# Layer 1's u and v by two levels of block products between layer 2's products, with weight factors read from DRAM and x kept there

## The chip, the cores and the metric

One Trainium2 chip, one core. The time is device microseconds (us) of one execution of the whole program, the median of three runs. Everything that is computed in matrix products here is fp32, except layer 3's sign products.

## The reference, cut to what matters

x is 8 images of 512 channels by 1024 pixels (32 x 32), and four layers follow one another. The change touches layer 1 and the order of layers 1 and 2.

```python
# layer 1, per image; h = group_norm(x), N = 1024, C = 512
q = wq h + bq ; k = wk h + bk ; v = wv h + bv
attn = softmax(q^T k / sqrt(C))          # over the 1024 keys
x = x + wp (v attn^T) + bp
# layer 2, per image: three 128-row projections t, p, g of x, softmax attention of
# t and p, then z = Z_w att, folded batch norm, x = x + z
```

The kernel folds weights: `wu` = wk^T wq, so that the scores of layer 1 are h^T u with u = wu h + bias (512 x 1024), and `wo` = (wp wv)^T, so that v = h^T wo (1024 x 512) already carries the output projection. u and v are thus one product each with a 512 x 512 matrix, per image.

## The kernel before

Before the main part, a start of some 210 us loads x, makes layer 0's small products for all images, layer 0's spectral norms (`chain`, a row of small dependent products for each pair of images) and the folded weights (`product`, `sums_of`, in a generator `filler` that is drawn on between the steps of the first chain). All that lives in SBUF pools `a1` and `a2`, which are closed there; the main part's pools (`late`, `big`, `epool`, `small`) lie over the same addresses. `big` is opened with `reuse_waits="tile"`; the others wait for the closed pools as a whole.

Then the images go one after the other through `fast`, in the order 6, 7, 0, 1, ... 5. In `fast(n)`:

- `scores1`: layer 1's scores h^T u, four calls of `seven`, exponentials, their sums `esum`. Between its steps the second half of the last image's layer 3 (`rest3`), then the load of the next x and layer 0 of the next image (`enter`), and steps of the remaining chains are drawn.
- `make_v`: v, two calls of `seven` with products of 128x256. After its fourth step `inverse_sums` makes the reciprocals of `esum`.
- `values1`: v times the exponentials, 14 groups of four products; in its middle the next image is normalised (`normal`) and split (`split_h`).
- `project2`, `scores2`, `values2`, `close2`, `leave`: layers 2 and 3. Between their steps `fill()` draws steps of `make_u` for the next image. `scores1` of the next image needs all of u and its sums.

All of the large products but layer 2's later ones go through `seven`: one level of Strassen's scheme in Winograd's form. It makes seven products of quarter matrices where eight are needed plainly. `sums_of` makes the left factors S1 to S4 from the quarters of one matrix, `differences_of` the right factors T1 to T4 from those of the other; the seven results are combined in PSUM evictions (DVE, ACT, and one POOL add in each `seven`).

PSUM is one ring of eight banks in the main part (`bank()`). x is double buffered in SBUF (two tiles of 16 KB per partition). `uv` is one 16 KB tile that holds u, then v. `wu`, `wo` and their sums `su`, `so` stay in SBUF (28 KB per partition). The order of each engine's instructions is written out when the program is built, by the tile framework, from the order in the source and its own estimate of when each becomes ready; on the chip each engine works off its list in order. A result that is late on the chip stops what is behind it.

Of the kernel before, what the change touches and what calls it, by code (L numbers as in the profile page):

```python
# [16 lines left out]
P = 128  # L17
B = 8
# [63 lines left out]

@with_exitstack
def kernel(
# [23 lines left out]
    xpool = ctx.enter_context(tc.tile_pool(name="x", bufs=2))  # L108
# [9 lines left out]
    def quad():  # L118
        return psum["bank"].tile([P, 4, P], F32, tag="bank", name="quad")

    def bank():
        return psum["bank"].tile([P, HF], F32, tag="bank", name="bank")

    def psum_pools(stack, wides, banks):
        psum.clear()
        for name, n in (("wide", wides), ("bank", banks)):
            if n:
                psum[name] = stack.enter_context(
                    tc.tile_pool(name=f"{name}{n}", bufs=n, space=PSUM, reuse_waits="tile")
                )  # L130

    def load_x(b):
        t = xpool.tile([P, CC, N], F32, tag="x", name="xt")
        src = x[b].rearrange("(cc p) n -> p cc n", p=P)
        for cc in range(CC):
            nc.sync.dma_start(out=t[:, cc, :], in_=src[:, cc, :])
        return t
# [108 lines left out]
    wu = wpool.tile([P, CC, C], F32, tag="wu", name="wu")  # L246
    wo = wpool.tile([P, CC, C], F32, tag="wo", name="wo")
# [4 lines left out]
    su = wpool.tile([P, 3, 2, C // 2], F32, tag="su", name="su")  # L252
    so = wpool.tile([P, 3, 2, C // 2], F32, tag="so", name="so")
# [39 lines left out]
    def sums_of(a, more):  # L293

        a11, a12, a21, a22 = a
        s1, s2, s4 = more
        tt = nc.vector.tensor_tensor
        tt(s1, a21, a22, ALU.add)
        tt(s2, s1, a11, ALU.subtract)  # L299
        tt(a21, a11, a21, ALU.subtract)  # L300
        tt(s4, a12, s2, ALU.subtract)
        return {"A11": a11, "A12": a12, "A22": a22, "S1": s1, "S2": s2, "S3": a21, "S4": s4}

    def differences_of(b, more):

        b11, b12, b21, b22 = b
        t1, t2, t4, t3 = (list(more) + [b12])[:4]
        tt = nc.vector.tensor_tensor
        tt(t1, b12, b11, ALU.subtract)
        tt(t2, b22, t1, ALU.subtract)  # L310
        tt(t3, b22, b12, ALU.subtract)
        tt(t4, b21, t2, ALU.subtract)
        return {"B11": b11, "B21": b21, "B22": b22, "T1": t1, "T2": t2, "T3": t3, "T4": t4}
# [45 lines left out]
    def product_of(lt, rhs, view=None, parts=1):  # L359

        def term(ps, ka, kb, first, last):
            fresh = ps is None
            if fresh:
                ps = bank()
            w = HF // parts
            for q in range(parts):
                for k in range(2):
                    mm(  # L370
                        out=ps[:, q * w : (q + 1) * w],
                        lhsT=lt(ka, kb, q, k),
                        rhs=rhs(ka, kb, q, k),
                        start=first and q == 0 and k == 0,
                        stop=last and k == 1,
                        skip_group_check=True,
                    )
            return ps, ps if view is None else view(ps)

        return term  # L380
# [72 lines left out]
    def make_u(env, hb, got):  # L453

        ut = env["big"].tile([P, CC, N], F32, tag="uv", name="ut")
        wa = weights["u"]

        def done():
            us = env["big"].tile([P, 3, 2, HF], F32, tag="us", name="us")
            got.append(  # L460
                sums_of(quarters_of(ut, chunks, [half(0), half(1)]), [us[:, i] for i in range(3)])
            )

        for i in range(2):
            term = product_of(
                lambda a, b, q, k: wa[a][:, k, bass.ts(i, P)],
                lambda a, b, q, k: hb[b][:, k, :],
            )
            yield from seven(
                term,  # L470
                ut[:, i, half(0)],
                ut[:, i, half(1)],
                ut[:, 2 + i, half(0)],
                ut[:, 2 + i, half(1)],
                bu[:, i : i + 1],
                bu[:, 2 + i : 3 + i],
                then=done if i else None,
            )

    def make_v(hb, vt):  # L480

        wa = weights["o"]
        w = C // 2
        for i in range(0, NTH, 2):
            term = product_of(
                lambda a, b, q, k: hb[b][:, k, bass.ts(i + q, P)],
                lambda a, b, q, k: wa[a][:, k, :],
                lambda ps: ps.rearrange("p (q c) -> p q c", q=2),
                2,
            )  # L490
            lo, hi = slice(i, i + 2), slice(NTH + i, NTH + i + 2)
            yield from seven(
                term, vt[:, lo, 0:w], vt[:, hi, 0:w], vt[:, lo, w:], vt[:, hi, w:]
            )

    def scores1(env, hb, ua, es):
# [3 lines left out]
        for i in range(NTH):  # L500
            lo, hi = (env["e"].tile([P, N], F32, tag="e", name="e") for _ in range(2))
            es[i], es[NTH + i] = lo, hi
            term = product_of(
                lambda a, b, q, k: hb[b][:, k, bass.ts(i, P)],
                lambda a, b, q, k: ua[a][:, k, :],
# [14 lines left out]
    def values1(env, xt, vt, es, r, more):  # L520
# [4 lines left out]
        w = C // 2  # L525
        a11, a12, a21, a22 = quarters_of(
            vt, [slice(0, NTH), slice(NTH, NT)], [slice(0, w), slice(w, C)]
        )
        s2 = more[:, 0, :].rearrange("p (t c) -> p t c", c=w)
# [5 lines left out]
        def group(ps, a, e, r_, first, last):  # L535
            for t in range(NTH):
                mm(  # L537
                    out=ps,
                    lhsT=a[:, t, bass.ts(r_, P)],
# [6 lines left out]
        def scaled(dst, oc, h):  # L546

            nc.vector.tensor_tensor(dst, dst, r[:, h, :], ALU.mult)
            xs = xt[:, oc, half(h)]
            nc.gpsimd.tensor_tensor(xs, xs, dst, ALU.add)  # L550
# [10 lines left out]
        pa = [bank(), bank()]  # L561
# [9 lines left out]
        for i in range(2):  # L571
            group(pa[i], a12, e21, i, False, True)
            d = temp(1)
            tt(d, pa[i], r[:, 0, :], ALU.mult)
# [7 lines left out]
        for i in range(2):  # L582
            pb = bank()
# [3 lines left out]
        pc = [bank(), bank()]  # L587
# [11 lines left out]
        pd = [bank(), bank()]  # L599
# [12 lines left out]
    def project2(env, xt, made):  # L612
# [11 lines left out]
        term = product_of(lambda a, b, q, k: wa[a][:, k, :], lambda a, b, q, k: xb[b][:, k, :])  # L624
# [194 lines left out]

    def fast(env, n, hb, ua):  # L820
# [3 lines left out]
        xt = resident.pop(b)  # L824
        more = n + 1 < B
        ahead = iter(())
# [8 lines left out]
        for k, _ in enumerate(scores1(env, hb, ua, es)):  # L835
            if rest3 and k % 2:
                if next(rest3[0], "end") == "end":
                    rest3.pop()
                    if more and order[n + 1] not in resident:
                        resident[order[n + 1]] = load_x(order[n + 1])  # L840
# [8 lines left out]
        vt = env["big"].tile([P, NT, C], F32, tag="uv", name="vt")  # L849
        for k, _ in enumerate(make_v(hb, vt)):  # L850
            if k == 3:
                r = inverse_sums(env, esum, n)
            chore(2)
        scratch = env["big"].tile([P, 3, N], F32, tag="us", name="scratch")
        got = []
        steps = iter(())
        for k, _ in enumerate(values1(env, xt, vt, es, r, scratch)):
            chore(2)
            if k == 5 and more:
                nxt = resident[order[n + 1]]  # L860
                hb = split_h(env, normal(env, nxt))
        signs = None
        if more:
            steps = make_u(env, hb, got)
# [8 lines left out]
        for k, _ in enumerate(project2(env, xt, made)):  # L873
            fill(k > 5)
        tt, pt, gt = made
        es, esum = scores2(env, pt, tt, lambda t: fill(t % 2))
        banks, r = [None, None], None

        def values2(h, ts):
            if banks[h] is None:  # L880
                banks[h] = bank()
# [16 lines left out]
        fill()  # L898
# [4 lines left out]
        values2(1, range(0, NTH))  # L903
        close2(xt, att, 0)
        att = values2(1, range(NTH, NT))
        count = iter(()) if more else count_bad(env)
        next(count, None)
        fill()
        for _ in leave(env, xt, dst, [0], signs):
            fill()  # L910
        close2(xt, att, 1)
        fill(2)
# [7 lines left out]
        return hb, got[0] if more else None  # L920
# [387 lines left out]

    def filler():
# [5 lines left out]
        cols2 = [slice(0, C // 2), slice(C // 2, C)]  # L1315
        weights["u"] = sums_of(quarters_of(wu, chunks, cols2), [su[:, i] for i in range(3)])
        scale_z()
        yield
        yield from biases()
        for j in rest:  # L1320
            yield from grams(j)
        yield from product(nat["v"], sbw["p"], wo)
        weights["o"] = sums_of(quarters_of(wo, chunks, cols2), [so[:, i] for i in range(3)])
# [33 lines left out]
    with ExitStack() as main:  # L1357
        psum_pools(main, 0, 8)
# [3 lines left out]
        env.update({"big": big, "e": epool, "small": small})  # L1362
        got = []
        hb = split_h(env, normal(env, resident[order[0]], True))
        for _ in make_u(env, hb, got):
            pass
        ua = got[0]
# [36 lines left out]
    def general(env, xt, b, dst):  # L1404
        for _ in enter(xt, load_f(b), weights0(b)):
            pass
        ht = normal(env, xt)
        ut = env["big"].tile([P, CC, N], F32, tag="u", name="u")
        vt = env["big"].tile([P, NT, C], F32, tag="v", name="v")
        for oc in range(CC):  # L1410
            for h in range(NH):
                ps = bank()
                for cc in range(CC):
                    mm(
                        out=ps,
                        lhsT=wu[:, cc, bass.ts(oc, P)],
# [5 lines left out]
        for t in range(NT):  # L1422
            ps = bank()
            for cc in range(CC):
# [3 lines left out]
                    rhs=wo[:, cc, :],  # L1428
# [58 lines left out]
    with tc.If(verdict[0] > 0):  # L1487
        with (
# [7 lines left out]

            for a in (weights["u"], weights["o"]):
                nc.vector.tensor_tensor(a["S3"], a["A11"], a["S3"], ALU.subtract)
# [45 lines left out]
```

## Time and profile before

| | |
|---|---|
| median of 3 runs | 1959.05 us (1958.59 to 1959.05) |
| the profiled execution: its time, its span | 1959.65 us, 1957.9 us |
| PE, weight loads, DVE, ACT, POOL busy | 1913.9, 989.2, 1151.2, 512.8, 223.9 us |
| one image in the middle (from one `values1` to the next, 784 to 997 us) | 212.4 us |
| DMA | 67.0 MB in all |

Line numbers such as L370 are those of the kernel before. L370 is the product inside `product_of`, so the products of u, v, layer 1's scores and layer 2's projections all carry it, and are told apart by the tiles they read. An fp32 product shows as two PE records. [...]the pace is read from a long row of them in the chain of waits, where a row of 112 records in 48.07 us is 0.429 us for each record.

### The profile page before, as it was taken

Reading aid. Unit: us, or ns where it says so; the run is one execution under the profiler, and the core shown is the slowest. Engines: PE = TensorE matmul, PEld = TensorE weight load, DVE = VectorE, ACT = ScalarE, POOL = GpSimd, SP = SyncE. Lnnn points to the kernel's source line nnn. Section 1 sums busy time; section 2 is a strip of 40 time slices with the busy share of each in tenths; the row PEclk is TensorE's granted clock in tenths of the full one; section 3 lists DMA queues with packets and bytes.
Section 4 is the critical chain, followed back from the end, with each engine's and each line's share of the span. In section 5 each row is a group of like instructions: output and inputs, shape, how many; then the busy total and the mean of one; then the engine's idle time right before and its main releaser. Section 6 shows DMA issues by size and latency. Waiting matters only on the chain.

```text
span 1957.9 us, 16696 instructions
## 1 busy us (share of the span) xinstructions
PE 1913.9 (98%) x6230; PEld 989.2 (51%) x6230; DVE 1151.2 (59%) x1859; ACT 512.8 (26%) x811; POOL 223.9 (11%) x176
## 2 busy tenths in 40 slices
PE   8999899999999999999999999999999999999997
PEld 2377347454565446454455446444645445544653
DVE  3245667537774487637754577447663775466546
ACT  2132122125220342024211332025202421134114
POOL 1000001300021001210112001200120011201110
PEclk9989899999999999999999999999999999999999
DMA  9320000002000020001100120002000110010001
GB/s 337 130 76 1 6 6 12 1 11 86 6 12 1 11 86 17 1 1 46 56 11 0 33 70 12 1 11 86 11 0 1 51 46 11 0 33 22 11 1 56
DMA packets 26712, 66.99 MB, mean 34 GB/s; under 512 B 3760, under 2 KB 4016, under 8 KB 25984
## 3 DMA queue, kind: packets, MB, share of 16 engines
q1 hardware_dynamic: 25968, 65.09, 9.8%
q8 instruction: 51, 0.84, 0.2%
q0 software_dynamic: 224, 0.33, 0.1%
q10 hardware_dynamic: 432, 0.43, 0.1%
q14 instruction: 37, 0.30, 0.0%
HBM read 38.51 MB, written 18.87 MB: 29 GB/s over the span
## 4 chain that ended last, share of the span: by engine, by line
PE 93%; DVE 3%; ACT 2%; DMA 0%; issue 0%; POOL 0%; DVEq 0%; ACTq 0%
PE bank L370 43%; PE bank L537 20%; PE bank L883 6%; PE bank L761 6%; PE bank L1131 4%; PE bank L638 3%; PE bank L655 3%; PE bank L393 2%; PE bank L675 1%; PE bank L935 1%; PE wide L1187 1%; PE bank L1241 1%; PE bank L936 1%; PE bank L782 1%; PE quad L1044 1%; ACT both L699 0%
## 5 line engine op out<-in xcount | busy, mean ns | idle before, releaser
L537 PE MATMUL bank<-e,vt 128*128 128x512 f32 x768 | 334.0, 593 | 0.0
L537 PEld LDWEIGHTS bank<-e,vt 128*128 128x128 f32 x768 | 145.0, 190 | 175.4 <-issue 173.1
L370 PE MATMUL bank<-ut,h 128*128 128x512 f32 x384 | 183.4, 598 | 4.7 <-ACT e L332 4.7
L327 DVE TENSOR_TENSOR e<-bank,e 128x512 f32<-128x512 f32 x128 | 87.6, 684 | 61.5 <-PE bank L370 60.2
L370 PE MATMUL bank<-us,hs 128*128 128x512 f32 x256 | 121.3, 596 | 0.5 <-DVE us L299 0.5
L370 PEld LDWEIGHTS bank<-ut,h 128*128 128x128 f32 x384 | 70.6, 190 | 87.7 <-issue 73.5
L883 PE MATMUL bank<-e,tpg 128*128 128x512 f32 x256 | 114.6, 595 | 0.0
L761 PE MATMUL bank<-tpg 128*128 128x512 f32 x256 | 114.6, 592 | 0.0
L768 ACT ACTIVATE e<-bank 128x512 f32<-128x512 f32 x128 | 76.4, 597 | 128.5 <-PE bank L761 128.5
L370 PE MATMUL bank<-h,wu 128*128 128x512 f32 x192 | 92.1, 603 | 4.9 <-DVE h L443 4.9
L370 PE MATMUL bank<-wo,h 128*128 128x256 f32 x384 | 91.9, 382 | 0.0
L773 DVE TENSOR_TENSOR esum<-esum,e 128x1024 f32<-128x1024 f32 x48 | 58.8, 1225 | 54.9 <-ACT e L768 54.9
L342 POOL TENSOR_TENSOR e<-e 128x512 f32<-128x512 f32 x32 | 41.6, 1301 | 432.2 <-ACT e L321 361.3
L327 DVE TENSOR_TENSOR vt<-bank,vt 128x512 f32<-128x512 f32 x64 | 44.0, 687 | 69.6 <-PE bank L370 69.3
L883 PEld LDWEIGHTS bank<-e,tpg 128*128 128x128 f32 x256 | 48.0, 190 | 63.9 <-issue 63.9
L761 PEld LDWEIGHTS bank<-tpg 128*128 128x128 f32 x256 | 48.6, 190 | 60.7 <-issue 60.5
L370 PEld LDWEIGHTS bank<-wo,h 128*128 128x128 f32 x384 | 71.6, 190 | 14.3 <-ACT vt L321 4.9
L342 POOL TENSOR_TENSOR ut<-ut 128x512 f32<-128x512 f32 x16 | 21.8, 1362 | 477.7 <-ACT ut L323 477.7
L370 PEld LDWEIGHTS bank<-us,hs 128*128 128x128 f32 x256 | 47.3, 190 | 57.5 <-issue 51.4
L790 DVE RECIPROCAL rsum<-bank 128x512 f32<-128x512 f32 x16 | 53.7, 3355 | 30.3 <-PE bank L782 30.3
L665 ACT ACTIVATE sg<-xt,rb 128x512 f16<-128x512 f32 x64 | 43.7, 717 | 103.7 <-DVE xt L657 100.9
L1131 PE MATMUL bank<-xt,fg 128*64 128x512 f32 x256 | 58.6, 608 | 5.3 <-DMA fg<-in_w_fg 5.3
(321 smaller groups left out, 3084.4 us busy)
## 6 DMA issues: line engine op xcount, KB each, us to landing
xt<-in_x SPq DMA_DIRECT2D x56, 512.0 KB
out<-both SPq DMA_DIRECT2D x64, 256.0 KB
rfull<-rsum SPq DMA_DIRECT2D x64, 128.0 KB
f_dram<-f SPq DMA_DIRECT2D x8, 256.0 KB
fb<-f_dram SPq DMA_DIRECT2D x8, 256.0 KB
w<-in_w SPq DMA_DIRECT2D x1, 1024.0 KB
q<-in_w_q SPq DMA_DIRECT2D x1, 1024.0 KB
k<-in_w_k SPq DMA_DIRECT2D x1, 1024.0 KB
```

What stands on the lines that cost most here:

```text
L327: nc.vector.tensor_tensor(dst, ps, u, ALU.add)
L342: nc.gpsimd.tensor_tensor(c22, c22, c12, ALU.add)
L370: mm(out=ps[:, q * w : (q + 1) * w], lhsT=lt(ka, kb, q, k), rhs=rhs(ka, kb, q, k), start=first and q == 0 and k == 0, stop=last and k == 1 ...
L537: mm(out=ps, lhsT=a[:, t, bass.ts(r_, P)], rhs=e[t], start=first and t == 0, stop=last and t == NTH - 1, skip_group_check=True,)
L638: mm(out=ps[:, i, :], lhsT=xt[:, cc, bass.ts(4 * h + i, P)], rhs=sbw["tpg"][:, cc, 2 * P : 3 * P], start=cc == 0, stop=cc == CC - 1,)
L655: mm(out=ps, lhsT=sbw["z"][:, bass.ts(oc, P)], rhs=att, start=True, stop=True)
L761: mm(out=ps, lhsT=pt[:, 0, bass.ts(t, P)], rhs=tt[:, 0, half(h)], start=True, stop=True,)
L768: nc.scalar.activation(e[:, half(h)], ps, AF.Exp, scale=float(P) ** -0.5)
L773: nc.vector.tensor_tensor(esum, esum, e, ALU.add)
L790: nc.vector.reciprocal(r, ps)
L883: mm(out=banks[h], lhsT=gt[:, t, :], rhs=es[t][:, half(h)], start=t == 0, stop=t == NT - 1,)
L1131: mm(out=banks[i][side(h), :], lhsT=w0[i][:, cc, :], rhs=xt[:, cc, half(h)], start=cc == 0, stop=cc == CC - 1,)
```

## The change

Seven things change together.

1. u and v are made by two levels of the seven-product scheme: seven `unit`s, each of seven `pieces`. A piece of u is one product of 128x256, a piece of v two of 128x128. That is 49 pieces each.
2. v of the next image is made where u is: `make_uv` replaces `make_u` and `make_v`, its 98 pieces are drawn between layer 2's products (`fill(3)`, `fill(4)`, `fill(8)`), units of u and v in turn. For the first image they are made alone (`together` is False), u first.
3. The seven times seven left factors of `wu` and `wo` are written to DRAM in the start (`factor`: 32 DVE operations and 22 DMAs for each matrix), and each unit reads its seven blocks (458 KB) back into one of three `wd` tiles. `wu`, `wo` now live in `a1`; SBUF keeps no weights of layer 1.
4. The right factors of the inner level are made on POOL, four subtractions of 128x256 for each of the seven outer factors, into one of two `hd` tiles; for the first image, separately for u and for v. A unit's seven results are gathered in a tile `pj` (one for u, one for v) and added to the outer result by operations of 128x1024: seven for u on DVE, seven for v on POOL, per image.
5. x goes to DRAM as soon as layer 0 has been added to it and `normal` is issued (2 MB, `leave_x`), and comes back before `values1` needs it. Three 16 KB places are passed round between x, u and v.
6. PSUM is two rings of four banks. Layer 2 takes ring 0, pieces take ring 1; in `scores1` the calls alternate.
7. `inverse_sums` of layer 1 moves from `make_v` to after the first group of `values1`; since no `make_v` stands between, `values1` follows on `scores1` directly. `values2` of the second half runs before `close2` of the first.

The diff, cut to its core:

```diff
-    xpool = ctx.enter_context(tc.tile_pool(name="x", bufs=2))
+    xpool = ctx.enter_context(tc.tile_pool(name="x", bufs=1))
...
-    def make_u(env, hb, got):
...
-    def make_v(hb, vt):
...
+    def place():
+        k = (next(places) + 2) % 3
+        pool = env["big"] if k == 2 else xpool
+        return pool.tile([P, CC, N], F32, tag=f"x{k}", name="place")
+
+    def pieces(env, name, j, hd, dst, bias):
+        wd = env["wd"].tile([P, len(FACTORS), P], F32, tag="wd", name="wd")
+        nc.sync.dma_start(out=wd, in_=factors[name][j])
...
+        def term(ps, ka, first, last):
+            ps = bank(1) if ps is None else ps
+            w, h = wd[:, index[ka], :], hd[FACTORS[ka]]
+            if name == "u":
+                parts = [(ps[:, 0 : 2 * P], w, h)]
+            else:
+                parts = [(ps[:, bass.ts(q, P)], h[:, bass.ts(q, P)], w) for q in range(2)]
...
+        c11, c12, c21, c22 = dst
+        pa = term(None, "A11", True, False)
+        nc.scalar.copy(c12, pa[:, 0 : 2 * P])
+        yield
+        plus(c12, term(None, "S2", True, True), None, c12)
+        yield
...
+    def make_uv(env, hb, together):
...
+        turns = ["A11", "S2", "S1", "S3", "A12", "S4", "A22"]
...
+                hd = env["wd"].tile([P, 4, 2 * P], F32, tag="hd", name="hd", bufs=2)
+                t = differences_of(
+                    [b[:, k, n * 2 * P : (n + 1) * 2 * P] for k in range(2) for n in range(2)],
+                    [hd[:, i, :] for i in range(4)],
+                    nc.gpsimd,
+                )
...
+            yield from pieces(env, name, j, differences(name, j), four(name, to), bias)
+            t = to.rearrange("p a b -> p (a b)")
+            add = (nc.vector if name == "u" else nc.gpsimd).tensor_tensor
+            if j == "S2":
+                add(c21, c11, t, ALU.add)
...
+        if together:
+            order_ = [("u", turns[0])]
+            for k, j in enumerate(turns):
+                if k + 1 < len(turns):
+                    order_.append(("u", turns[k + 1]))
+                order_.append(("o", j))
...
-            if k == 5 and more:
-                nxt = resident[order[n + 1]]
-                hb = split_h(env, normal(env, nxt))
+            if k == 5 and more:
+                hb = leave_x(env, n + 1)
...
-            steps = make_u(env, hb, got)
+            steps = make_uv(env, hb, True)
...
-            fill(k > 5)
+            fill(3)
...
-        es, esum = scores2(env, pt, tt, lambda t: fill(t % 2))
+        es, esum = scores2(env, pt, tt, lambda t: fill(3))
...
+    def factor(name, w):
+        nc.sync.dma_start(out=plain[name], in_=w)
+        sums = a1.tile([P, 4, 2, C // 2], F32, tag="sums", name="sums")
...
+        for i, j in enumerate(FACTORS):
...
+            to = factors[name][j]
+            nc.sync.dma_start(out=to[:, 0:2, :], in_=a[:, :, 0:P])
+            nc.sync.dma_start(out=to[:, 2, :], in_=a[:, 1, P : 2 * P])
+            nc.sync.dma_start(out=to[:, 3:7, :], in_=m)
...
-        weights["u"] = sums_of(quarters_of(wu, chunks, cols2), [su[:, i] for i in range(3)])
+        factor("u", wu)
...
-        weights["o"] = sums_of(quarters_of(wo, chunks, cols2), [so[:, i] for i in range(3)])
+        factor("o", wo)
...
-        psum_pools(main, 0, 8)
+        psum_pools(main, 0, 4, 4)
...
+        wd = main.enter_context(tc.tile_pool(name="wd", bufs=3))
```

## The prediction

> **What bounds the kernel now.** First the engines' shares on the page, then the chain of work that ended last.
>
> ```profile
> PE 1913.9 (98%) x6230; PEld 989.2 (51%) x6230; DVE 1151.2 (59%) x1859; ACT 512.8 (26%) x811; POOL 223.9 (11%) x176
> PE 93%; DVE 3%; ACT 2%; DMA 0%; issue 0%; POOL 0%; DVEq 0%; ACTq 0%
> ```
>
> PE sets the time, and nothing waits long. Third, the chain in order of time (start, us, what): one image.
>
> ```profile
> 784.15 48.07 PE bank L537 x112
> 832.22 13.73 PE bank L370 x32
> 845.95 3.57 PE bank L638 x32
> ...
> 979.11 17.46 PE bank L370 x80
> 996.57 48.07 PE bank L537 x112
> ```
>
> One image takes 996.57 - 784.15 = 212.4 us. Rows give the pace of a record (two per product): 48.07/112 = 0.429 us at 512 columns, 17.46/80 = 0.218 at 256 (L370, v), 3.57/32 = 0.112 at 128. So PE is paced by columns, and narrow products lose 2 to 4%. Fourth, busy times by stretch (PE, PEld, DVE, ACT, POOL, clock, DMA share, GB/s): layer 2 with the next u, the whole image, and a stretch in which x is loaded.
>
> ```profile
> 832.00:923.00 91.00, 90.32 (x268) 43.42 (x267) 47.01 (x57) 29.76 (x47) 6.51 (x5) 1.00 0.06 18
> 784.00:997.00 213.00, 211.61 (x615) 105.67 (x614) 128.55 (x176) 56.58 (x87) 26.89 (x18) 1.00 0.08 26
> 480.00:485.00 5.00, 3.20 (x11) 1.64 (x11) 4.54 (x11) 3.09 (x6) 0.00 (x0) 1.00 0.95 352
> ```
>
> PE idles 1.4 us per image; DVE has 40% left, POOL nearly all. Fifth, the timeline where the start hands over to the main part.
>
> ```profile
> 202.90 1.22 DVE L1198 COPY wo<-wide 128x1024 f32<-128x1024 f32 x1
> ...
> 211.15 3.75 PE L370 MATMUL bank<-h,wu 128*128 128x512 f32 x4 [4.86 <-DVE h L443]
> ...
> 238.70 1.88 PE L370 MATMUL bank<-ut,h 128*128 128x512 f32 x4
> ```
>
> `wo` is complete at 204.1; PE is already idle then, as the first image's statistics run on DVE, and the first u product starts at 211.15. The first u takes until 238.7. Last, POOL and DVE additions (min/median/max ns; then busy, mean ns, idle before).
>
> ```profile
> L342 POOL TENSOR_TENSOR vt<-vt x16: 1262/1266/2049, 309.3 to 1830.7; 128x512 f32<-128x512 f32 x16
> L558 DVE TENSOR_TENSOR scratch<-e 128x512 f32<-128x512 f32 x32 | 21.4, 681 | 0.0
> L581 DVE TENSOR_TENSOR e<-e,scratch 128x512 f32<-128x512 f32 x32 | 28.9, 943 | 0.2 <-PE bank L537 0.2
> ```
>
> [...]the POOL add goes from 1.26 to 2.05 us, and L581, which runs while POOL adds to x, takes 943 ns where L558 of the same shape takes 681.[...]
>
> **Part by part.**
>
> *PE, u and v.* Before, each image: u 28 products of 512 = 56 x 0.429 = 24.0 us; v 56 of 256 = 112 x 0.218 = 24.4. After: u 49 of 256 = 98 x 0.218 = 21.4; v 98 of 128 = 196 x 0.112 = 21.9. Saved 48.4 - 43.3 = **5.2 us** an image. Seven images are made between layer 2's products: **-36 us**. The first is counted below.
>
> *DVE in layer 2.* Adds 14 units x 5 evictions of 128x256 at 0.41 us (the nearest row, the 128x256 sums of `tpg`) = 28.7, and 7 x 1.22 (the 128x1024 sums of `us`) = 8.5; removes u's 8 evictions at 0.7 = 5.7. So 47 + 31.5 = 78.5 us beside PE's 91 - 24 + 43.3 = 110 us: 71%, some 10% more where POOL blocks it. Not the bound, but cover shrinks. ACT gains some 3 us; no bound.
>
> *POOL.* 28 subtractions x 0.72 + 7 adds x 2.34 = 36.6 us per image, 50 if blocked half of the time: under half of 110 us. But it stands on the path at one place: there are two `hd` tiles, so the four subtractions for factor j+2 start only when v's pieces of factor j are over, and the second piece of u's next unit needs the second of them. That is 0.72 x 2 + 0.2, or 4.0 us if the 2.34 us add of v's last unit slips between. PE has one piece (0.44 us) and whatever layer 2 product is listed next (0.86 or 1.7 us). Six turnovers per image, seven images: 42.
>
> *DMA and SP.* Each image adds 14 `wd` loads of 458 KB and 4 MB of x: 10.4 MB at the 352 GB/s above is 30 us of 207, and 22 issues at 0.44 us on SP's queue. `wd` has three tiles, so a load may be two units (about 2 x 110/14 = 16 us) ahead; even behind a 2 MB x (6 us) it lands. I price it at nothing; if SP stood on a late output, a whole unit's pieces and all PE work listed behind them would wait, some 4 us each.
>
> *Between layer 1's two halves.* `make_v` was 24 us of PE in which DVE finished `esum`, its reciprocal (3.35 us) and the broadcast DMAs. Now `values1` follows at once. The first four groups (13.7 us) need none of it; DVE must make 2 `esum` adds, 8 small sums, one 1024-wide sum and the reciprocal by then, about 12 us. It fits barely, not in images that also carry a chain.
>
> *Stalls.* No row shows these. Bounds: nothing, up to 8 us an image (one 1.2 us stop per turnover). I take 1.5 us an image, **+10 us** (0 to 56), since layer 2 products can fill most of it.
>
> *The start.* (a) `factor("u")` has 28 more DVE operations of 128x128 at 0.2 to 0.3 us, 6 to 8 us, in a stretch where DVE is idle 53 of 115 us, but the chain and the transposes need DVE in turn: +2 (-1 to +7). (b) `factor("o")` can begin only at 204.1. The `wd` pool lies over the last tiles of `a1` and `a2` and waits for both as a whole, so the first weights come in after all of its writes: 4.2 MB, 12 us at 352 GB/s[...] (22 issues at 0.44 are 9.7 us). I take 16, plus 2.5 for the landing and 2.5 for the `wd` load: first piece at 225 instead of 211.15, **+14** (8 to 24). (c) The first u alone is bound by its evictions and the 1.2 us add into one `pj`: about 4.3 us a unit, 30.5 us where it took 27.5 (+3); v is paced by POOL (7 x 5.2 = 36 us), with the first scores as filler, and the 4 us gap before `us` goes: -2. Together +1 (-4 to +8). Sum of the start: **+17** (+5 to +35).
>
> *The end.* The last image has no pieces; ring 0 alone could cost it 0 to 2 us. Nothing taken.
>
> **Sum:** -36 + 17 + 10 = -9 us. Against the profiled execution's 1959.65 us (span 1957.9 and 1.75 around it) that is 1950.6; the median lies 0.6 lower, so **1950 us**.
>
> **Rivals.**
>
> 1. *Slower: the turnover of the `hd` tiles.* PE stands still at the second piece after each turnover, because v's add is taken ahead of the subtraction on POOL and the layer 2 products have already been used up. From -36 + 17 = -19, the change loses more than 0.2% once each of the 42 stops costs over 23/42 = 0.55 us. With the 4.0 us above less 0.44 and one product of 1.7 it could be 1.2 to 1.9; at 1.2, +50: about 1990 us. For: POOL goes from 27 to some 63 us an image, and the profile shows it slowed by DVE. Against: on average eleven layer 2 products (67 us / 7 / 0.86) lie between two turnovers.
> 2. *Faster by more: the start costs nothing.* If the writes of `factor("o")` are not waited for, or scores fill the gap, -36 + 2 + 6: about 1931 us. For: idle PE at 204 to 211 exists already. Against: the pool rule above.
> 3. *Even.* Start at its upper end (33) with few stalls (+4): about 1960 us.
> 4. *It doesn't save what it says.* If weight loads pace the 128-column pieces (a row of L638 shows PEld busy at 0.116 us a record), v takes 22.8 us and 29 us are saved instead of 36; that alone moves the forecast to 1957.
>
> **How the numbers follow.** 0.2% (4 us) is what a measurement of this kernel can tell from no change. Forecast 0.38 and rival 2 0.15 give faster 0.53. Rivals 3 and 4 give same 0.12. Rival 1 with its milder forms gives slower 0.35. Both signs hold most: the forecast's own range is 1936 to 1957; the whole range, cut where a tenth is left on each side, is 1928 to 1994.
>
> **What the changed profile would show.** Right: records of 256 and 128 columns at 0.218 and 0.112 in long rows; a period of about 208 us between two `values1`; first piece near 225, released by a DMA into `wd`; DVE near 72% in layer 2, POOL near 45%. Wrong: PE idle before pieces with POOL's `hd` as the releaser (rival 1), with DMA `wd` in the middle of images (SP's order), or DVE as the releaser in `values1`; or a first piece near 211.

## The result, and the profile after

| | before | after |
|---|---|---|
| median | 1959.05 us | 2055.61 us (4 runs, 2051.59 to 2058.31) |
| ratio, 95% interval | | 1.0491 [1.0472, 1.0509] |
| profiled execution: time, span | 1959.65, 1957.9 us | 2051.59, 2049.8 us |
| start: first product of the first `values1` | 330.1 us | 353.9 us |
| the seven stretches from one `values1` to the next | 1505.0 us | 1571.9 us |
| rest | 122.8 us | 124.0 us |

The change makes the kernel 4.9% slower. The forecast was 1950 us, and its range ended at 1994. The spans differ by 91.9 us: 23.8 in the start, 66.9 in the seven stretches (forecast: a gain of 26), 1.2 at the end. A middle image takes 216 to 221 us where it took 211 or 212; the first two stretches, which also carry a chain of layer 0, grow by 14.2 and 17.0 us, the five others by 5.6 to 8.4. Line numbers below are those of the kernel after: L493 is the product of a piece, L505, L507 and L511 its evictions, L328 to L331 the four differences on POOL, L581 to L589 the additions of a unit to the outer result, L385 the old `seven`'s product.

The engines' shares and the chain of work that ended last, from the page:

```profile
PE 1921.6 (94%) x7238; PEld 1066.3 (52%) x7238; DVE 1400.8 (68%) x2403; ACT 537.2 (26%) x939; POOL 545.1 (27%) x452
PE 73%; DVE 13%; POOL 7%; ACT 4%; issue 3%; DMA 0%; DVEq 0%; SPq 0%; POOLq 0%; ACTq 0%
```

No engine but PE is over 70% busy, yet the chain that was 93% PE is now 73%: DVE, POOL and ACT hold the end in turns. DMA and SP are not on it. PE's waits by releaser (total us, times, longest):

```profile
PE bank L493 <- POOL hd L329: 37.0, 25, 12.7
PE bank L493 <- ACT pj L511: 15.5, 13, 5.4
PE bank L385 <- ACT e L351: 11.9, 5, 2.4
```

POOL's differences come first. 12.7 us of that line are the wait before the very first piece, which reads `h` and `wd` only; in no_pool_work, below, the same 12.7 us are put down to the `wd` load. In the seven stretches 21 waits are left, 22.7 us in all and 2.4 us at most: three in each image. Of the second line 6.1 us lie in the stretches and 9.4 in the start. POOL is behind part of it: over the whole run the ACT copy into `pj` (L511) stood 71 us for POOL's additions that read `pj` (L585, L589), ten times. In all, PE idles 72.1 us in the seven stretches where it idled 11.2. The shares in layer 2 of a middle image (PE, PEld, DVE, ACT, POOL, clock, DMA share, GB/s):

```profile
1312.00:1434.00 122.00, 117.31 (x495) 73.58 (x494) 82.18 (x123) 33.79 (x64) 37.03 (x31) 1.00 0.19 59
```

DVE is at 67% and POOL at 30%: both lower shares than forecast (71% and 45%). DVE's 82.2 us are more than the 78.5 that were expected, but they lie in a longer stretch. PE still idles 4.7 us in it. What it waits for, in order of time (start, duration, what, then idle time and releaser):

```profile
1365.04 0.72 POOL L328 TENSOR_TENSOR hd<-h 128x256 f32<-128x256 f32 x1 [15.54 <-PE bank L493]
1365.24 0.60 PE L493 MATMUL bank<-h,wd 128*128 128x256 f32 x2
1365.34 1.51 DVE L887 TENSOR_TENSOR esum<-esum,e 128x1024 f32<-128x1024 f32 x1
1365.72 1.71 POOL L330 TENSOR_TENSOR hd<-h 128x256 f32<-128x256 f32 x1
1367.39 0.72 POOL L329 TENSOR_TENSOR hd<-h,hd 128x256 f32<-128x256 f32 x1
1368.17 1.56 PE L493 MATMUL bank<-hd,wd 128*128 128x256 f32 x6 [0.61 <-POOL hd L329]
1368.87 2.35 POOL L581 TENSOR_TENSOR place<-place,pj 128x1024 f32<-128x1024 f32 x1
1369.32 2.99 DVE L887 TENSOR_TENSOR esum<-esum,e 128x1024 f32<-128x1024 f32 x1
```

POOL was idle for 15.5 us and could not begin: both `hd` tiles were in use until PE's last piece of v. Then its second difference took 1.71 us instead of 0.73, while DVE's `esum` addition ran beside it, and PE stood for 0.61 us, until 1368.17. Next it is the other way round: POOL adds, and the next `esum` takes 2.99 us instead of 1.22; the two evictions behind it on DVE come late. This is one turnover (a tile is given back and filled again), with waiting and mutual slowing in the same 7 us. At the end of layer 2 the chain of waits shows another form:

```profile
1442.58 2.37 POOL place L589
1444.97 2.27 DVE place L673
...
1456.70 0.48 ACT e L351
1457.18 0.04 issue
1457.22 5.41 PE bank L385 x8
```

L673 is the first step of `values1` on v. It stands early in DVE's list and waits for POOL's last addition; behind it wait layer 3's operations, which hold ACT, which holds the scores. PE comes back at 1457.22 after 2.4 us; it stands so in five of the seven stretches.

The handover from the start, for comparison with the lines of before:

```profile
205.01 1.22 DVE L1333 COPY wo<-wide 128x1024 f32<-128x1024 f32 x1
...
217.67 0.32 SPq L481 DMA_DIRECT2D wd<-factor_uA  x1
217.84 0.17 DVE L1507 MEMSET ones<- 128x128 f32 x1 [2.88 <-DMA factor_oS<-more]
...
221.14 1.19 PE L493 MATMUL bank<-h,wd 128*128 128x256 f32 x2 [12.73 <-POOL hd L329]
...
284.34 2.35 POOL L586 TENSOR_TENSOR place<-place 128x1024 f32<-128x1024 f32 x1
...
284.72 1.22 PE L493 MATMUL bank<-wd,h 128*128 128x128 f32 x4 [5.42 <-ACT pj L511]
```

The first piece runs at 221.14 instead of 211.15. The first v, made alone, then goes at POOL's pace, a unit each 5.7 us, and PE waits up to 5.4 us inside it.

### The profile page after: what moved, and what is told of

It is laid out like the page before. It is cut to its first block, busy times and chain, and to the rows that moved or that the text cites. A ratio compares the mean times of both kernels' runs of the same rounds, so it can differ in the third digit from the quotient of the medians.

```text
span 2049.8 us, 20515 instructions
## 1 busy us (share of the span) xinstructions
PE 1921.6 (94%) x7238; PEld 1066.3 (52%) x7238; DVE 1400.8 (68%) x2403; ACT 537.2 (26%) x939; POOL 545.1 (27%) x452
## 4 chain that ended last, share of the span: by engine, by line
PE 73%; DVE 13%; POOL 7%; ACT 4%; issue 3%; DMA 0%; DVEq 0%; SPq 0%; POOLq 0%; ACTq 0%
PE bank L385 19%; PE bank L651 15%; PE bank L493 13%; PE bank L1008 5%; PE bank L1266 4%; PE bank L875 4%; PE bank L752 3%; PE bank L769 2%; POOL place L589 2%; POOL hd L330 2%; PE bank L408 2%; POOL hd L329 1%; ACT both L813 1%; POOL hd L328 1%; DVE pj L505 1%
## 5 line engine op out<-in xcount | busy, mean ns | idle before, releaser
L651 PE MATMUL bank<-e,place 128*128 128x512 f32 x768 | 340.6, 597 | 0.3 <-ACT o_b L705 0.3
L651 PEld LDWEIGHTS bank<-e,place 128*128 128x128 f32 x768 | 143.7, 191 | 171.2 <-issue 165.7
L505 DVE TENSOR_TENSOR pj<-bank,pj 128x256 f32<-128x256 f32 x328 | 138.1, 422 | 121.4 <-PE bank L493 74.1
L385 PE MATMUL bank<-place,h 128*128 128x512 f32 x384 | 192.1, 614 | 12.6 <-ACT e L351 11.9
L493 PE MATMUL bank<-hd,wd 128*128 128x256 f32 x448 | 128.5, 397 | 32.1 <-POOL hd L329 24.3
L493 PEld LDWEIGHTS bank<-wd,hd 128*128 128x128 f32 x896 | 118.5, 194 | 46.7 <-issue 19.7
L493 PE MATMUL bank<-wd,hd 128*128 128x128 f32 x896 | 129.2, 281 | 3.4 <-DVE pj L505 3.0
L361 POOL TENSOR_TENSOR e<-e 128x512 f32<-128x512 f32 x32 | 41.8, 1306 | 334.1 <-ACT e L340 265.4
L385 PE MATMUL bank<-us,hs 128*128 128x512 f32 x256 | 125.5, 602 | 2.9 <-DVE us L318 2.9
L493 PEld LDWEIGHTS bank<-hd,wd 128*128 128x128 f32 x448 | 83.1, 195 | 79.2 <-POOL hd L329 36.8
L385 PEld LDWEIGHTS bank<-place,h 128*128 128x128 f32 x384 | 70.4, 195 | 84.8 <-issue 65.1
L328 POOL TENSOR_TENSOR hd<-h 128x256 f32<-128x256 f32 x36 | 28.8, 800 | 281.7 <-PE bank L493 260.2
L589 POOL TENSOR_TENSOR place<-place,pj 128x1024 f32<-128x1024 f32 x24 | 57.1, 2377 | 139.9 <-DVE pj L505 139.9
L511 ACT COPY pj<-bank 128x256 f32<-128x256 f32 x80 | 29.7, 371 | 242.4 <-PE bank L493 155.3
L505 DVE TENSOR_TENSOR place<-bank,place 128x256 f32<-128x256 f32 x160 | 66.8, 421 | 29.6 <-PE bank L493 23.1
```

Of the source, the lines that this page charges most:

```text
L385: mm(out=ps, lhsT=lt(ka, kb, k), rhs=rhs(ka, kb, k), start=first and k == 0, stop=last and k == 1, skip_group_check=True,)
L493: mm(out=to, lhsT=lt, rhs=rhs, start=first and q == 0, stop=last, skip_group_check=True,)
L505: nc.vector.tensor_tensor(to, ps[:, 0 : 2 * P], u, ALU.add)
L589: add(c, c, t, ALU.add)
L651: mm(out=ps, lhsT=a[:, 2 * r_ + t // 2, bass.ts(t % 2, P)], rhs=e[t], start=first and t == 0, stop=last and t == NTH - 1, skip_group_check ...
```

## The experiments

Four theories were weighed. **Late results**: PE waits for what POOL makes (differences through two `hd` tiles, v's additions through `pj` and DVE's list). **DVE's load**: the evictions and additions of the second level are too much for DVE. **The arrangement**: weights and x through DRAM, two rings of banks, v between layer 2's products, no gap before `values1`. **Interference**: operations of POOL and DVE take longer beside one another (in before POOL's add goes from 1.26 to 2.05 us), whoever waits for the results. The medians, against 1959.0 us for the kernel before, with the time of the first `values1` and the sum of the seven stretches:

| kernel | us | ratio, 95% interval | first `values1` | seven stretches |
|---|---|---|---|---|
| before | 1959.05 | | 330.1 | 1505.0 |
| after | 2055.61 | 1.0491 [1.0472, 1.0509] | 353.9 | 1571.9 |
| no_inner_diff | 2000.84 | 1.0206 [1.0189, 1.0223] | 341.0 | 1538.0 |
| no_v_add | 1990.52 | 1.0161 [1.0144, 1.0178] | 341.3 | 1522.6 |
| no_pool_work | 1945.42 | 0.9930 [0.9913, 0.9947] | 334.4 | 1484.4 |
| one_level | 1955.59 | 0.9983 [0.9976, 0.9990] | 323.1 | 1506.3 |
| v_add_on_dve | 2030.99 | 1.0367 [1.0350, 1.0384] | 345.1 | 1549.7 |
| all_on_dve | 2002.72 | 1.0220 [1.0203, 1.0237] | 351.9 | 1526.1 |
| hd_three | 1996.31 | 1.0194 [1.0176, 1.0213] | 348.8 | 1522.2 |
| pool_busy | 2035.53 | 1.0390 [1.0373, 1.0408] | 346.8 | 1563.1 |
| pool_unread | 2132.97 | 1.0885 [1.0867, 1.0903] | 346.7 | 1659.1 |
| first_in_turns | 2046.19 | 1.0442 [1.0424, 1.0459] | 347.4 | 1575.9 |
| hd_three_first | 1995.02 | 1.0191 [1.0174, 1.0208] | 343.4 | 1520.8 |
| pool_on_weights | 2007.42 | 1.0246 [1.0221, 1.0271] | 347.4 | 1530.9 |

The last two columns are from one profiled execution of each kernel. The executions of one version with POOL's work lie up to 12 us apart (2001.1 to 2011.1 us for pool_on_weights, 2021.1 to 2032.7 for v_add_on_dve), and the profiled one of v_add_on_dve was 9.9 us below its median, so differences of a few us between these rows carry no weight.

### What POOL's work costs: no_inner_diff, no_v_add, no_pool_work

The inner differences are left out (no_inner_diff; plain blocks of h stand in their place), v's outer additions (no_v_add), or both (no_pool_work). Here and in the three kernels with spare work below, the branch at the end that computes everything again in another way is never taken:

```diff
-                hd = env["wd"].tile([P, 4, 2 * P], F32, tag="hd", name="hd", bufs=2)
-                t = differences_of(
...
-                    nc.gpsimd,
+                b11, b12, b21, b22 = (
...
+                t = {"B11": b11, "B21": b21, "B22": b22}
+                t.update({"T1": b12, "T2": b22, "T3": b12, "T4": b21})
...
             direct = {"A11": 0, "S1": 3}
+            if name == "o":
+                direct = {"A11": 0, "S1": 3, "S2": 2, "S4": 1}
...
+            if name == "o":
+                return
             if j == "S2":
...
-    with tc.If(verdict[0] > 0):
+    with tc.If(verdict[0] > 100):
```

> Leaves out the 28 inner subtractions per image that POOL makes into the hd tiles (T1 to T4 are replaced by plain blocks of h), so a piece waits for no POOL result and POOL loses 20 us an image; the fallback branch at the end isn't taken. Theory A (POOL's results come late and hold PE): most of the 97 us goes, to some 1985 us, with the stretch from the first piece to the first scores (80 us in the changed kernel) down to about 60 and an image in the middle (216.4 us) at 212 or less. Theory B (DVE has too much to do): little changes, 2040 us or more. Theory C (the new arrangement: two rings, v moved, x through DRAM): little changes, 2040 us or more.

> Leaves out the additions of v's units to the outer result (as in no_pool_work), keeps the inner subtractions on POOL; the fallback branch isn't taken. Without the subtractions the additions cost 55 us (2000.8 against 1945.4). If PE's waits for the hd tiles alone cost as much as the additions do, about 2000 us; if the cost comes from the additions standing ahead of the subtractions in POOL's line, the subtractions alone are nearly free: below 1965 us.

> Leaves out both: the inner subtractions, and the five additions of v's units to the outer result (two units more write their block directly, three write pj and are not added). POOL then has no more to do than before the change; DVE keeps its 35 evictions for u and for v and the seven additions for u. Theory A: 1950 us or a little above, below 1975. Theory B: still over 2020 us. Theory C: still over 2020 us.

Each half of POOL's work is worth about half: 55 us for the differences, 65 for the additions, 110 for both. With neither, the kernel is faster than before, and a middle image takes 206.9 or 208.6 us instead of 210.8 or 212.4. PE's products are the same in number and shape (7238 records in all). So a saving is there, and POOL's part in the change costs 110 us, though POOL is 27% busy.

### The arrangement alone: one_level

All of the new order (v between layer 2's products, two rings, x through DRAM, three places, `inverse_sums` later), but u and v with one level of the scheme, as before, and the weights kept in SBUF:

```diff
-        wd = main.enter_context(tc.tile_pool(name="wd", bufs=3))
...
+                        lhsT=wu_[ka][:, k, bass.ts(i, P)],
+                        rhs=hb[kb][:, k, :],
...
-            fill(3)
+            fill()
```

> The changed kernel's arrangement (v of the next image between layer 2's products, two rings of four banks, x to DRAM and back, three places, inverse_sums inside values1) with the single level of products of the kernel before: no factors, no wd or hd or pj tiles, weights in SBUF. Nothing is left out. Theories A and B: the arrangement costs little, about 1965 us (1955 to 1985). Theory C: most of the 97 us stays, over 2020 us.

Its stretches sum to 1506.3 us, those of before to 1505.0. The arrangement costs nothing, v's place and x's way through DRAM included. The way of the weights through DRAM isn't in this kernel; it is in no_pool_work, where PE waits for no `wd` load after the first piece. The start of one_level is 7.0 us shorter; the cause of that was not tried. This is the only complete version below the kernel before, by 3.5 us, about the bound of what can be told from no change.

### Moving POOL's work to DVE: v_add_on_dve, all_on_dve

```diff
-            add = (nc.vector if name == "u" else nc.gpsimd).tensor_tensor
+            add = nc.vector.tensor_tensor
```

all_on_dve also has `nc.vector` instead of `nc.gpsimd` for the inner differences.

> The seven 1024-wide additions of v per image go from POOL (2.35 us each) to DVE (1.22 us each); nothing is left out. Theory A: pj is free 1.1 us sooner after each unit of v and POOL's line is shorter, so 20 to 40 us are gained, to about 2020 us. Theory B: DVE gets 8.5 us more per image and the time rises, to about 2070 us. Theory C: no change, 2050 us.

> Inner subtractions and v's additions both on DVE (0.41 us and 1.22 us each where POOL takes 0.72 and 2.35); nothing is left out. POOL does only what it did before the change, DVE gets 28 x 0.41 + 7 x 1.22 = 20 us more per image, on 168 busy us of some 210. If POOL's slowness and its place in the order is the cause (A), the time falls below v_add_on_dve's 2031, to 1970 to 2000 us; if DVE's load is (B), it rises above 2055.

Both are faster than after, neither is near 1945. With all of it on DVE (1486.7 us busy, 74%) no wait of PE for POOL is left and the kernel is still 57 us over the one that does none of this work: 17.5 in the start and 41.8 in the seven stretches. The two `hd` tiles are still there: PE waits 13.3 us in the stretches, once an image, for the differences that DVE now makes. So a late result can come from DVE as well; how much of the rest is DVE's load as such was not tried.

### A third `hd` tile: hd_three

On top of v_add_on_dve; a `wd` tile is given up for the room:

```diff
-                hd = env["wd"].tile([P, 4, 2 * P], F32, tag="hd", name="hd", bufs=2)
+                hd = env["wd"].tile([P, 4, 2 * P], F32, tag="hd", name="hd", bufs=3)
...
-        wd = main.enter_context(tc.tile_pool(name="wd", bufs=3))
+        wd = main.enter_context(tc.tile_pool(name="wd", bufs=2))
```

> v_add_on_dve (2031 us) with three hd tiles instead of two, for which wd goes from three tiles to two; nothing is left out. If the turnover of the hd tiles is what holds PE (the subtractions of a factor can then start a unit of v earlier), below 2000 us; if POOL's or DVE's amount of work is, 2020 to 2035 us.

It takes 35 us off v_add_on_dve, and PE's waits show why. In v_add_on_dve the wait for POOL's differences is 44.5 us in 25 times, 30.1 us of it in the seven stretches; here it is:

```profile
PE bank L493 <- POOL hd L329: 0.4, 1, 0.4
```

In the profiled executions the seven stretches are 27.5 us shorter for it. The turnover of the `hd` tiles is shown as a cause by this. A middle image is at 209.7 to 213.6 us, no better than before the change; the two stretches with a chain of layer 0 are 4.6 and 14.7 us over before.

### POOL as busy, nobody waits: pool_busy, pool_unread, pool_on_weights

Three kernels start from no_pool_work and give POOL its work back without a reader, to part waiting from interference. The first two failed at that, each in its own way.

pool_busy lets POOL's spare operations read v's blocks:

```diff
+                if j in direct:
+                    spare = env["wd"].tile([P, 4 * 2 * P], F32, tag="hd", name="spare", bufs=2)
+                    for i in range(7):
...
+                        nc.gpsimd.tensor_tensor(spare[:, 0 : 2 * P], a, b, ALU.subtract)
+                    for i in range(1 + (j != "A11")):
+                        nc.gpsimd.tensor_tensor(spare, t, t, ALU.add)
```

> no_pool_work (1945 us) with the same amount of POOL work as the changed kernel has (28 subtractions of 256 and 7 additions of 1024 columns per image), made from the blocks of v into a tile that nobody reads; the same parts of the computation are left out. If the cost of POOL's work is that others wait for its results, below 1955 us; if it is that POOL and DVE block one another's reads, over 1980 us.

Its 2035.5 us hold a new wait. DVE's first step of `values1` overwrites a block that the spare work still reads (the chain of waits):

```profile
1362.68 1.90 POOL spare L588
1364.58 0.02 issue
1364.61 1.23 DVE place L683
```

Here it stood at the head of DVE's list from 1357.75, in the middle of layer 2, and PE's next piece ran at 1367.41, after standing for 5.8 us; so it goes in each of the seven stretches. No data that PE needs came from POOL.

pool_unread makes the true differences, in the true tiles, and lets the products read plain blocks; the additions read only h:

```diff
+                b11, b12, b21, b22 = (
+                    b[:, k, n * 2 * P : (n + 1) * 2 * P] for k in range(2) for n in range(2)
+                )
+                t = {"B11": b11, "B21": b21, "B22": b22}
+                t.update({"T1": b12, "T2": b22, "T3": b12, "T4": b21})
...
+                for i in range({"A11": 0, "S1": 1, "S3": 2}.get(j, 1)):
+                    spare = env["wd"].tile([P, 2, HF], F32, tag="hd", name="spare", bufs=2)
+                    nc.gpsimd.tensor_tensor(spare, hb["B11"], hb["B21"], ALU.add)
```

> POOL does the same work in the same places as in the changed kernel, 28 inner subtractions of 128x256 into the hd tiles and seven additions of 128x1024 for each image, but nothing reads what it makes: the inner products take plain blocks, v's seven outer additions are left out of the result, and POOL's additions read only the normalised input, which nobody overwrites for long. Without any of POOL's work the kernel takes 1945.4 us, with all of it 2055.6. If the time goes in waits for POOL's results, this kernel is near 1945 to 1955 us. If POOL's mere use of SBUF beside DVE costs it (operations of both that block one another), it is 2000 us or more. In between, each has its part: the distance to 1945 is the interference, the distance to 2056 the waiting.

Neither theory gave 2133 us. With no reader, nothing spaced the work: all 28 differences and seven additions of an image became ready at once when h was there, and POOL's list has them in one row (the timeline of POOL, its first and its last lines):

```profile
1335.38 0.73 POOL L328 TENSOR_TENSOR hd<-h 128x256 f32<-128x256 f32 x1 [2.02 <-DVE h L458]
...
1374.97 2.34 POOL L590 TENSOR_TENSOR spare<-h 128x1024 f32<-128x1024 f32 x1
1377.26 1.26 POOL L676 TENSOR_TENSOR place<-place,o_a 128x512 f32<-128x512 f32 x1
```

`values1`'s first addition to x (L676) stood behind it from 1348.1, when DVE had made its `o_a`, to 1377.26; DVE's `o_b` waited for the tile that they read, and PE for DVE (115 us in five waits).

pool_on_weights lets the spare work read the unit's weight tile, which comes at most two units ahead; this spaces it over layer 2:

```diff
...
+            for i in range(4):
+                nc.gpsimd.tensor_tensor(
+                    spare[:, i, :].rearrange("p (a b) -> p a b", a=2),
+                    wd[:, 0:2, :],
+                    wd[:, 2:4, :],
+                    ALU.subtract,
+                )
...
+                    for k in range(2):
+                        nc.gpsimd.tensor_tensor(
+                            spare[:, 2 * k : 2 * k + 2, :].rearrange("p a (c b) -> p (a c) b", c=2),
+                            wd[:, 0:4, :],
+                            wd[:, 3:7, :],
+                            ALU.add,
+                        )
```

> Left out, as in the kernel without POOL's work: the inner differences (plain blocks stand in their place) and v's seven outer additions. In their place POOL does the same amount in each image, 28 subtractions of 128x256 and, for each addition of 128x1024, two of 128x512, all of which read the unit's weight tile, which is loaded at most some two units ahead; so POOL's list stays spread over layer 2 as in the changed kernel, nothing reads what it makes, and only the load into a weight tile three units later waits for it. Without POOL's work the kernel takes 1945.4 us, with it in use 2055.6. If the loss is waiting for POOL's results, this kernel is at 1945 to 1965 us. If it is POOL and DVE blocking one another at SBUF, it is at 2000 us or more.

2007.4 us: 62.0 above no_pool_work and 48.2 below after. 13.0 us of the 62.0 lie in the start, and they are not interference: DVE waits there for 13.0 us, once, for a step of layer 0's chain on POOL (`root`) that stands behind the spare work. The seven stretches are 46.5 us above no_pool_work. In them PE and ACT wait for POOL nowhere and DVE as long as in no_pool_work (26 us in both), and PE, ACT and DVE run the same operations in the same order as there, but for one DVE operation that has moved by one place in the start. PE waits for a `wd` load once after its first piece, 1.2 us. Its POOL is 569.2 us busy (545.1 after). DVE's instructions are the same 2403 as in no_pool_work, but take 1407.6 us instead of 1349.5. PE's waits (the same two are nil in no_pool_work), and then DVE's groups of one shape:

```profile
PE bank L503 <- DVE pj L515: 17.3, 13, 2.1
PE bank L503 <- DVE place L515: 14.1, 13, 2.3
```

```profile
L911 DVE TENSOR_TENSOR esum<-esum,e 128x1024 f32<-128x1024 f32 x48 | 72.1, 1502 | 5.8 <-ACT e L906 5.8
L515 DVE TENSOR_TENSOR pj<-bank,pj 128x256 f32<-128x256 f32 x248 | 104.1, 420 | 50.6 <-PE bank L503 40.0 <-ACT pj L521 3.0
L825 DVE TENSOR_SCALAR both<-both 128x512 f32<-128x512 f32 x28 | 18.1, 648 | 2.6 <-ACT both L824 2.6
```

The same rows in no_pool_work:

```profile
L890 DVE TENSOR_TENSOR esum<-esum,e 128x1024 f32<-128x1024 f32 x48 | 58.5, 1219 | 7.6 <-ACT e L885 7.6
L505 DVE TENSOR_TENSOR pj<-bank,pj 128x256 f32<-128x256 f32 x248 | 104.8, 422 | 48.5 <-PE bank L493 39.4 <-ACT pj L511 1.5
L804 DVE TENSOR_SCALAR both<-both 128x512 f32<-128x512 f32 x28 | 11.8, 421 | 1.7 <-ACT both L803 1.7
```

The eviction, with one operand in PSUM, takes 420 ns with POOL at work and 422 without. `esum`, with both in SBUF, goes from 1219 to 1502 ns. The third row shows that the number of inputs in SBUF alone doesn't decide: it is a `tensor_scalar` with one, and goes from 421 to 648 ns. The rows show that these operations take longer, not by what; the cause was not shown. The evictions themselves take no longer; that they are late since they stand behind slowed operations in DVE's list is what the chain of waits suggests, and was not tried apart.

### The first image: first_in_turns, hd_three_first

```diff
-        for _ in make_uv(env, hb, False):
+        for _ in make_uv(env, hb, True):
```

hd_three_first has this edit and those of hd_three.

> Nothing is left out. The first image's u and v are made with their units in turns, as for the other images, so that the inner differences are made once for both (28 POOL subtractions instead of 56), and POOL's addition for a unit of v lies beside the next unit of u. If the start is held by POOL's 5.7 us for each unit of v made alone, its some 80 us from the first piece to the first scores shrink to about 60 and the total to 2035 to 2045 us, all of it before the first values1. If the start's loss lay in the factors' way through DRAM alone, the time stays at 2050 to 2058.

> Nothing is left out. All repairs of the two-level arrangement together: three hd tiles (and two of wd), v's outer additions on DVE, and the first image's units in turns. Three hd tiles with the additions on DVE gave 1996.3 us, of which the start before the first values1 is 19 us over the kernel before. If the waits for POOL were what the change lost, this comes to 1978 to 1990 us; it stays above the kernel before (1959) as long as DVE, which the two levels load most, sets the pace of the images that also carry a chain of layer 0. If DVE's load costs nothing, it comes below 1959.

Making the first u and v in turns brings the first `values1` forward by 6.5 us, less than expected; the rest of the start stays. All repairs together give 1995.0 us, not told apart from hd_three's 1996.3 and above the range that was expected: in two levels, no version that does all the work came near the kernel before.

## Why the prediction was wrong

**The sum.** It had -36 for PE, +10 for stalls, +17 for the start. Measured on the spans: +66.9 where -36 + 10 stood, +23.8 where +17 stood.

**PE's saving: right.** Rows of pieces run at 0.217 us a record (1.30 us for 6) and 0.112 (1.34 us for 12). Without POOL's work the seven stretches lose 20.6 us, where 26 were forecast with the stalls, and a middle image 2.5 to 3.9: roughly the 5.2 us less the 1.5 taken for stalls. Of the two stretches with a chain one loses 3.1 us and the other gains 0.5. Rival 4 (pieces paced by weight loads) fell.

**Stalls, +10: the term that failed.** In the stretches POOL's work costs 1571.9 - 1484.4 = 87.5 us, 12.5 an image (16.5 and 17.3 in the two stretches with a chain, 9.5 to 11.3 in the others), above the bound of 8 in each. pool_on_weights splits it: 46.5 us come with POOL's work while nobody in the stretches waits for its results, which leaves the slowing of DVE, and the other 41.0 come when the results are used. This split rests on one kernel whose POOL work is of the same amount but reads other tiles, and its executions lie 10 us apart, so the parts are rough; the 41.0 are a rest, in which the lists are also ordered otherwise. How the 46.5 us divide over the single slowed operations was not tried. Both parts hold a cost that the prediction had nowhere: after some of PE's stops the tensor clock is granted at 0.50, in the seven stretches for some 31 us in after, 10 in pool_on_weights and never in no_pool_work, by estimate up to 15 and 5 us lost.

**The step behind it.** The prediction saw the interference in the trace (681 to 943 ns, 1.26 to 2.05 us), wrote "Not the bound, but cover shrinks" and put nothing for it into the sum, since DVE would be at 71%. DVE was at 67%, and the interference cost about as much as the waits. An `esum` that takes 2.99 us instead of 1.22 is no load; it is a delay in a list that also holds the evictions, one for each 0.44 us piece, on a ring of four banks.

**Rival 1: right in kind, too small.** It put the stop at the second piece after a turnover, and the point of decision at 0.55 us for each of 42. The trace has 21 such waits in the seven stretches, 1.1 us each, 22.7 us in all; with v's additions on DVE they are 30.1 us, and hd_three removes these and 27.5 us of the stretches. The prediction had v's addition in layer 2 only as something that delays a subtraction. It also holds `pj` (PE waits 6.1 us for the copy into it) and, through L673, DVE's whole list (11.9 us before the scores, in five stretches).

**The start: +17, measured +23.8, by other terms.** (a) `wo` is copied 2.1 us later, as taken. (b) The first piece came 10.0 us later, so 7.9 for the writes instead of 14. The 16 us for the writes and the 2.5 each for landing and load were the author's estimate; from the end of `wo`'s copy at 206.23 to the issue of the first `wd` load at 217.67 it took 11.4 us, and the piece ran 3.5 us after that. (c) The first u and v were put at +1, with scores as filler; they cost 13.8. The pace of POOL had been seen (5.2 us a unit, 5.7 measured; the 0.72 and 2.34 us in it, for operations that before doesn't have, were the author's estimate, and after shows 0.73 and 2.35 where they run undisturbed), but the filler did not fill: of the scores 18 records ran before the last piece of v. Without POOL's work the whole start is +4.3. (The prediction gives the upper end of the start as 35 in one place and as 33 in rival 3; with 35 that rival would stand at 1962.)

**Priced at nothing, rightly:** DMA and SP (no wait for a `wd` load in the middle of an image in after), the closed gap before `values1` and x's way through DRAM (one_level), the end (+1.2).

## What to carry to other kernels

An engine's busy share doesn't tell what work on it costs: POOL at 27% cost 110 us of 2056; in the seven stretches, roughly half of its cost came with late results and half without anyone waiting for them, while DVE's `esum` additions, with two SBUF inputs, took 1502 ns instead of 1219. When a change saves PE time by more additions, price each as a delay in the lists that also hold PE's evictions, and before writing it, time the kernel with those additions left out and with them made but unread. A buffer of two whose refill is made only after the last use can be a wait at a turn, here at three of six in each image; and work with no reader is not free, since it can stand in one row ahead of work that has one.

## What the runs showed of the hardware

The tensor clock fell after some short stops of PE and not after others. After the 2.4 us in which PE stood before 1457.22, the granted clock is at half from 1458.0 on for 3.4 us, and eight records took 5.41 us where 8 x 0.429 = 3.43 is the pace, so the stop cost another 2 us. In the seven stretches of after PE stood nine times for 2.37 or 2.38 us, and a window of 3.4 us at half clock began within about 1 us of five of these stops' ends; after the other four, and after the three stops of 1.8 us before a piece, none did. In the stop before 1457.22 the gap between products was 2.4 us and the one between weight loads 3.2; what decides whether the clock falls was not shown. After the turnover's stop of 0.61 us at 1368 the next row of 12 records ran at 0.112 us. The mean clock was 0.991 before, 0.98 after, and 0.953 in pool_unread, where PE stood up to 24 us at a time.
